# The first batch's third product: from four tile products to one product of seven blocks

## The chip, the cores and the metric

The kernel runs on one core of one Trainium2 chip. The metric is the device time of one execution in microseconds (us); the median over several runs is compared. The core's engines work side by side, each through its own instructions in order: TensorE (PE, matrix products into PSUM; PEld is its loading of the stationary operand), VectorE (DVE), ScalarE (ACT), GpSimd (POOL) and SyncE (SP), whose queue here issues nearly all DMAs. An instruction waits at the head of its engine's queue until what it needs is done, and everything behind it waits too.

## The reference, cut to what matters

The whole is one transformer block over 4 batches of 512 tokens of width 512: a layer norm, then attention and a mixture of experts on the normalised rows, both added to the input. The change touches only the shared expert, which every token passes through:

```python
def _expert_ffn(x, w1, wg, w2):
    return jax.nn.silu(x @ w1) * (x @ wg) @ w2
output = _expert_ffn(x, Ws1, Wsg, Ws2)
...
x = L0_attn_x
xn = _layernorm(x, axis=-1)
x = x + _L0_attn_ref(xn, ...) + _L0_ffn_ref(xn, ...)
```

All three matrices are 512 x 512 in float32. For one batch each product is a 512 x 512 by 512 x 512 product. The third one, by Ws2, is the one that the change does in another way, and only for the first batch.

## The kernel before, in words

**Order.** A planner places instructions on each engine. Those wrapped in `keep(...)` stay in the order in which the program writes them, engine by engine; the others are placed where the planner's own estimate of time finds them ready, the earlier written one first. Nearly all of TensorE's and VectorE's work in this stretch is kept. The sums of weight blocks on POOL (`gadd`, `gsub`, L959 and L962) and the additions of `product_y` (L868) are not.

**Loads.** SyncE loads a 128-token tile of x, Ws1, a second tile, Wsg, the third and fourth tile, Ws2, and then the four tiles of the second batch. The tiles go into `acc`, which also collects the result. `wbuf` holds the three matrices.

**The first batch** is done tile by tile, so that work can begin on the first 128 tokens. `norm(g, 1)` normalises a tile on VectorE (with one square root on ScalarE); POOL copies it into another layout (`xp`, L495), SyncE stores that to `xn_d` in DRAM (L501); TensorE transposes it and ScalarE copies it into `xnT` (L524, L525). Then `ffn_in` (L142) multiplies by Ws1 (tile h) and by Wsg (tile g), ScalarE takes Silu of h (L153), VectorE multiplies by g (L157, `at_s`), and `ffn_out` (L164) multiplies by Ws2 in four matmuls of 512 columns (`y_s`), which VectorE adds to `acc` (L828).

Between h and g of a tile, `between` writes work for later: for tiles 1 and 2 the transpose of the next tile and the normalisation of batch 1 or 2 as a whole: statistics, four scalings (L499), four stores to `xn_d`, and, behind them on SyncE's queue, four loads back in turned order (`xq`, L511). For tile 3 it is the statistics of batch 3 and `turn_batch(1)`, four transposes on VectorE from `xq` into `xnT` (L519). All of it is kept, so on VectorE it stands ahead of the tile's own multiplication at L157. `y_s` of a tile is written behind h and g of the following tile; that of the last tile is a hook behind the third product of `product_h("s1")`.

**The other batches** use seven products of blocks in place of eight. `seven` (L230) takes 2 x 2 blocks of both operands; `first_factors` and `second_factors` form four sums of one operand's blocks each, so that seven products (four matmuls of 256 columns each) suffice. They run in ORDER 0, 1, 5, 4, 6, 2, 3 into three PSUM banks. After products 0, 5, 4 and 6 ScalarE copies a bank out (L297); the others are read from the bank. `product_h` and `product_g` do the first two products of a batch, `product_y` the third, whose seven parts are added to `acc` by POOL (copied ones) and VectorE (banks). A `hooks` entry is called behind the product of that number. `tokens(b)` gives a batch's four sums from `xnT` on VectorE (L841) in parts; `feature_factors` and `weight_factors` give those of the matrices, on POOL here. The fourth sum of each set is written over a block of the matrix itself, so it waits for the last reader of that block.

**Around the change** the order written is: four tiles; POOL's sums of Ws1; the token sums of batch 1; the scaling of batch 3; `turn_batch(2)`; `product_h("s1")` with the last tile's third product inside; POOL's sums of Wsg and Ws2; `turn_batch(3)`; `product_g("s1")` with the start of the routing; and so on.

Of the kernel before, what the change touches and what calls it, by code (L numbers as in the profile page):

```python
# [10 lines left out]
F32 = mybir.dt.float32  # L11
# [7 lines left out]
P = 128  # L19
B, S, D = 4, 512, 512  # L20
NT = B * S
NTT = NT // P
TPB = S // P
# [4 lines left out]
FC = FF // P  # L28
# [14 lines left out]
def kernel(  # L43
# [38 lines left out]
    nc = tc.nc  # L82
    keep = tc.keep_in_program_order
# [15 lines left out]
    acc = const.tile([P, NTT, D], F32, tag="acc", name="acc")  # L99
    xnT = const.tile([P, DC, NT], F32, tag="xnT", name="xnT")  # L100
# [19 lines left out]
    sw = moe.enter_context(tc.tile_pool(name="sw", bufs=1, side="right"))  # L120
# [10 lines left out]
    def rows(src):  # L131
        return src.rearrange("(c p) f -> p c f", p=P)

    def ffn_in(at, name, w, x_of, between, step=FC):

        hp = fps.tile([P, S], F32, tag="h", name=f"h_{name}")
        gp = fps.tile([P, S], F32, tag="g", name=f"g_{name}")
        for ps, wt in ((hp, w[0]), (gp, w[1])):
            for f in range(FC):
                for c in range(DC):  # L140
                    keep(
                        nc.tensor.matmul(  # L142
                            ps[:, ts(f, P)],
                            wt[:, c, ts(f, P)],
                            x_of(c),
                            start=(c == 0),
                            stop=(c == DC - 1),
                        )
                    )
            if ps is hp:  # L150
                between()
        sl = sw.tile([P, S], F32, tag="v", name=f"sl_{name}", bufs=5)
        keep(nc.scalar.activation(sl, hp, AF.Silu))  # L153
        cols = [t.rearrange("p (c n) -> p c n", c=FC) for t in (gp, sl)]

        for f in range(0, FC, step):
            keep(nc.vector.tensor_mul(*(t[:, f : f + step] for t in (at, *cols))))  # L157
        return at

    def ffn_out(name, at_t, w, fix=lambda ins: None):  # L160
        yp = fps.tile([P, D], F32, tag="y", name=f"y_{name}")
        for f in range(FC):
            fix(
                nc.tensor.matmul(  # L164
                    yp, at_t[:, f, :], w[2][:, f, :], start=(f == 0), stop=(f == FC - 1)
                )
            )
        return yp
# [39 lines left out]
    def first_factors(add, sub, a11, a12, a21, a22, s1, s2, s4, s3):  # L208
        add(s1, a21, a22)
        sub(s2, s1, a11)  # L210
        sub(s4, a12, s2)
        sub(s3, a11, a21)
        return a11, a12, s4, a22, s1, s2, s3

    def second_factors(sub, b11, b12, b21, b22, t1, t2, t4, t3):
        sub(t1, b12, b11)
        sub(t2, b22, t1)
        sub(t4, b21, t2)
        sub(t3, b22, b12)
        return b11, b21, b22, t4, t1, t2, t3  # L220
# [49 lines left out]
    V, G = nc.vector, nc.gpsimd  # L270

    def block(t):
        if len(t.shape) > 2:
            axes = " ".join("abc"[: len(t.shape) - 1])
            t = t.rearrange(f"p {axes} -> p ({axes})")
        return t.rearrange("p (j f) -> p j f", j=2)

    def blocks(t):

        return [[t[:, 2 * k : 2 * k + 2, half[n]] for n in range(2)] for k in range(2)]  # L280
# [7 lines left out]
    def product(name, tag, a, w, done, hooks):  # L288

        banks = banks_of(tag, name)

        def kept(i, k):
            t = sw.tile([P, D], F32, tag="v", name=f"v{i}_{name}", bufs=5)
            keep(nc.scalar.copy(block(t), banks[k]))  # L297
            return block(t)

        copies = {0: (1, 0), 5: (2, 0), 4: (5, 2), 6: (3, 0)}  # L300
        sums = {1: 1, 2: 2, 3: 0}

        def then(p):
            if p in copies:
                done(copies[p][0], kept(*copies[p]))
            else:
                done(-p, banks[sums[p]])
            if p in hooks:
                hooks[p]()

        seven(a, w, banks, then, keep)

    def product_h(name, at, a, w, hooks={}, fix=lambda ins: None, more=G):

        (c11, c12), (c21, c22) = blocks(at)
        v = {}

        def silu(*blocks):
            for c in blocks:
                keep(nc.scalar.activation(c, c, AF.Silu))  # L320

        def done(i, src):
            v[i] = src
            if i == -1:
                fix(V.tensor_add(c11, src, v[1]))
            elif i == 3:
                silu(c11)
                fix(more.tensor_add(c22, v[3], v[5]))
            elif i == -2:
                fix(V.tensor_add(c12, src, v[2]))  # L330
            elif i == -3:
                silu(c12, c22)
                keep(nc.scalar.activation(c21, src, AF.Silu))

        product(f"h{name}", "h", a, w, done, hooks)
# [28 lines left out]
    def act_tile(name):  # L364
        return sw.tile([P, FC, S], F32, tag="at", name=f"at_{name}")

    def feature_factors(i, add, sub):

        (a11, a21), (a12, a22) = blocks(wbuf[i])
        return first_factors(add, sub, a11, a12, a21, a22, *wsum[i], a21)  # L370

    def weight_factors(sub):
        (b11, b12), (b21, b22) = blocks(wbuf[2])
        return second_factors(sub, b11, b12, b21, b22, *wsum[2], b12)
# [72 lines left out]
    with tc.tile_pool(name="rt", bufs=1) as rt, tc.tile_pool(name="fwork", bufs=2) as fw:  # L447
# [4 lines left out]
        def load_x(g):  # L452
            keep(nc.sync.dma_start(acc[:, g, :], x_f[ts(g, P), :]))
# [366 lines left out]
        shared = wbuf  # L820

        def shared_in(g, between):
            at = fw.tile([P, FC, P], F32, tag="at1", name=f"at_s{g}")
            return ffn_in(at, f"s{g}", shared, lambda c: xnT[:, c, ts(g, P)], between)

        def shared_out(g, at, fix=lambda ins: None):
            yp = ffn_out(f"s{g}", at, shared, fix)
            fix(nc.vector.tensor_add(acc[:, g, :], yp, acc[:, g, :]))  # L828

        def tokens(b):  # L830

# [22 lines left out]
        def parts_of(b):  # L854
            it = tokens(b)
            return lambda: next(it)

        def product_y(b, a, w, hooks={}, fix=lambda ins: None):
            def c(t, n):
                g = b * TPB + 2 * t  # L860
                return acc[:, g : g + 2, half[n]]

            to = {1: c(0, 0), -1: c(0, 0), 2: c(0, 1), -2: c(0, 1)}
            to.update({5: c(1, 1), 3: c(1, 1), -3: c(1, 0)})

            def done(i, src):
                eng = G if i > 0 else V
                fix(eng.tensor_add(to[i], src, to[i]))  # L868

            product(f"ys{b}", "y", a, w, done, hooks)  # L870

        def load(dst, src):
            keep(nc.sync.dma_start(dst, src))
# [3 lines left out]
        load(shared[0], rows(ws1))  # L877
        load_x(1)
        load(shared[1], rows(wsg))
        load_x(2)  # L880
        load_x(3)
        load(shared[2], rows(ws2))
        for g in range(TPB, 2 * TPB):
            load_x(g)


        warm = fps.tile([P, TPB, P], F32, tag="y", name="warm")
# [12 lines left out]
        for t, n, step, mul in (  # L900
# [3 lines left out]
                t, pattern=[[step, n]], base=S if t is by512 else 0, channel_multiplier=mul,  # L904
# [33 lines left out]
        def between():  # L938
            if t + 1 < TPB:
                turn_x(t + 1, tiles[t + 1])  # L940
                xq[t] = norm(t * TPB, TPB)
            else:
                stats[3] = statistics(3 * TPB, TPB)
                turn_batch(1, xq.pop(1))

        stats = {}
        at, xq = None, {}
        for t in range(TPB):
            nxt = shared_in(t, between if t else between_0)
            if at is not None:  # L950
                shared_out(t - 1, at, keep)
            at = nxt
        parts = routing()

        def route():
# [5 lines left out]
        def gsub(*t):  # L961
            return G.tensor_sub(*t)  # L962

        fs_h = feature_factors(0, gadd, gsub)
        x_of = parts_of(1)
        x_of()
        x_of()
        x1 = x_of()
        xq[3] = scaled(3 * TPB, TPB, *stats[3])
        turn_batch(2, xq.pop(2))  # L970
        last_tile = lambda: shared_out(TPB - 1, at, keep)
        at_1 = act_tile("s1")
        product_h("s1", at_1, fs_h, x1, {5: last_tile})
        fs_g = feature_factors(1, gadd, gsub)
        fs_y = weight_factors(gsub)
        turn_batch(3, xq.pop(3))
        for s in range(SURE, NUNIT):
            to = y_d[ts(s, S), :].rearrange("(t p) (c f) -> p t c f", p=P, f=P)
# [2 lines left out]
        x_of = parts_of(2)  # L981
# [11 lines left out]
        x_of = parts_of(3)  # L993
# [386 lines left out]
    with tc.If(used < SURE + 1) as few:  # L1380
        at = act_tile("few").rearrange("p c (t f) -> p t c f", t=TPB)[:, 0]
        at = ffn_in(at, "few", wbuf, lambda c: xT[SURE][:, c, :P], nothing, 1)
        y = sw.tile([P, D], F32, tag="v", name="y_few", bufs=5)
        yp = ffn_out("few", at, wbuf, keep)
# [395 lines left out]
```

## Time and profile before

| | us |
|---|---|
| median of 14 runs | 1340.39 |
| lowest and highest | 1339.82, 1342.11 |
| the profiled execution's own time | 1340.54 |
| its span in the profile | 1338.8 |
| TensorE busy | 1329.6 |
| VectorE busy | 971.3 |
| POOL busy | 847.4 |
| ScalarE busy | 405.8 |

Times in the profile are counted from the start of the span. A row of the timeline has the start, the length, the engine, the line of the kernel, the operation, what is written and read, and the count; in brackets the engine's idle time ahead of it and what ended that. `P` is 128. A matmul of float32 stands in the rows as two records, so a group of four matmuls has x8. The stretch that the change touches is roughly the first 70 us of the span.

### The profile page before, as it was taken

Reading aid. Unit: us, or ns where it says so; the run is one execution under the profiler, and the core shown is the slowest. Engines: PE = TensorE matmul, PEld = TensorE weight load, DVE = VectorE, ACT = ScalarE, POOL = GpSimd, SP = SyncE. Lnnn points to the kernel's source line nnn. Section 1 sums busy time; section 2 is a strip of 40 time slices with the busy share of each in tenths; the row PEclk is TensorE's granted clock in tenths of the full one; section 3 lists DMA queues with packets and bytes.
Section 4 is the critical chain, followed back from the end, with each engine's and each line's share of the span. In section 5 each row is a group of like instructions: output and inputs, shape, how many; then the busy total and the mean of one; then the engine's idle time right before and its main releaser. Section 6 shows DMA issues by size and latency. Waiting matters only on the chain.

```text
span 1338.8 us, 17913 instructions
## 1 busy us (share of the span) xinstructions
PE 1329.6 (99%) x5949; PEld 993.9 (74%) x5949; DVE 971.3 (73%) x1426; ACT 405.8 (30%) x714; POOL 847.4 (63%) x952
## 2 busy tenths in 40 slices
PE   9999999999999999999999999999999999999998
PEld 8778888888888888877655666667666666666676
DVE  7669486676767677676458679877788777897775
ACT  3333222322223322212223423323333323233231
POOL 5113664564545465532277789888898888988883
PEclk9999999999999999999999999999999999999999
DMA  7850356866667675523401331243322333213332
GB/s 280 191 159 19 93 134 158 220 180 185 186 169 203 165 228 162 157 92 98 147 16 45 110 111 32 89 132 110 110 60 69 124 111 110 76 58 120 110 110 87
DMA packets 174100, 167.90 MB, mean 125 GB/s; under 512 B 57904, under 2 KB 136752, under 8 KB 174000
## 3 DMA queue, kind: packets, MB, share of 16 engines
q1 hardware_dynamic: 161264, 133.10, 34.1%
q0 software_dynamic: 12736, 33.57, 8.7%
q8 instruction: 49, 0.80, 0.3%
q14 instruction: 51, 0.42, 0.1%
HBM read 116.02 MB, written 34.87 MB: 113 GB/s over the span
## 4 chain that ended last, share of the span: by engine, by line
PE 96%; DVE 2%; ACT 1%; DMA 0%; issue 0%; SPq 0%; POOL 0%; DVEq 0%; ACTq 0%; POOLq 0%
PE op L230 15%; PE hr L230 11%; PE av L1513 11%; PE yr L230 11%; PE gr L230 9%; PE sb L1432 4%; PE sa L1432 4%; PE pq L1297 4%; PE gs L230 3%; PE sa L1443 3%; PE ys L230 2%; PE pqr L1282 2%; PE hs L230 2%; PE sb L1443 2%; PE sb L1532 2%; PE h_s L142 1%
## 5 line engine op out<-in xcount | busy, mean ns | idle before, releaser
L182 POOL DMA_INDIRECT xs<-xn_d,idx_i x208 | 230.0, 1106 | 193.7 <-DVE xT L199 134.6
L1469 POOL TENSOR_TENSOR pt<-pt,tri 128x128 f32<-128x128 f32 x256 | 139.6, 566 | 68.9 <-ACT pt L1465 62.2
L1465 ACT ACTIVATE pt<-pt 128x512 f32<-128x512 f32 x160 | 94.4, 628 | 257.9 <-DVE pt L1461 256.9
L1513 PEld LDWEIGHTS av<-pt,xnT 128*128 128x128 f32 x512 | 95.5, 190 | 83.6 <-issue 47.7
L1513 PE MATMUL av<-pt,xnT 128*128 128x512 f32 (+3 forms) x512 | 149.8, 436 | 0.0
L230 PE MATMUL op<-m,og 128*128 128x256 f32 x512 | 118.6, 380 | 0.5 <-DVE og L1566 0.5
L1271 DVE TENSOR_TENSOR swap_q<-qraw,sinT 32x512 f32<-32x512 f32 x128 | 117.7, 919 | 1.7
L1497 POOL TENSOR_TENSOR su<-su,pt 128x256 f32<-128x256 f32 (+1 forms) x128 | 105.2, 822 | 10.0
L230 PEld LDWEIGHTS op<-m,og 128*128 128x128 f32 x512 | 96.1, 190 | 14.4 <-DVE og L1566 1.3
L1461 DVE TENSOR_SCALAR pt<-sa 128x512 f32<-128x512 f32 x64 | 41.1, 682 | 70.7 <-PE sa L1443 70.7
L1664 POOL DMA_INDIRECT yg<-y_d,pos_i x48 | 54.4, 1134 | 56.7 <-issue 50.3
L230 PE MATMUL op<-m,s 128*128 128x256 f32 x384 | 88.2, 379 | 0.1
L1497 POOL TENSOR_TENSOR su<-pt 128x384 f32<-128x384 f32 x64 | 83.8, 1310 | 0.0
L1612 POOL TENSOR_TENSOR acc<-acc,v 128x512 f32<-128x512 f32 x60 | 80.6, 1344 | 5.1 <-ACT v L1605 3.2
L230 PEld LDWEIGHTS op<-m,s 128*128 128x128 f32 x384 | 73.0, 190 | 10.2 <-issue 0.5
L1677 DVE SCALAR_TENSOR_TENSOR acc<-yg,wk,acc 128x512 f32<-128x512 f32 x48 | 56.7, 1181 | 19.1 <-POOL acc L1612 17.9
L1605 ACT COPY v<-op 128x512 f32<-128x512 f32 x64 | 37.5, 585 | 108.3 <-PE op L230 107.1
L1566 DVE TENSOR_TENSOR og<-og,rb 128x512 f32<-128x512 f32 (+1 forms) x68 | 68.5, 1068 | 0.6 <-PE rb L1552 0.2
L1615 DVE TENSOR_TENSOR acc<-op,acc 128x512 f32<-128x512 f32 x48 | 31.7, 686 | 49.5 <-POOL acc L1612 47.3
L230 PE MATMUL yr<-w,at_r 128*128 128x256 f32 x288 | 67.1, 381 | 0.5 <-DVE at_r L351 0.2
L230 PE MATMUL gr<-xT,w 128*128 128x256 f32 x288 | 66.1, 379 | 0.0
L230 PE MATMUL hr<-xT,w 128*128 128x256 f32 x288 | 66.1, 379 | 0.0
(339 smaller groups left out, 2809.4 us busy)
## 6 DMA issues: line engine op xcount, KB each, us to landing
m<-m_d SPq DMA_DIRECT2D x112, 256.0 KB, 5.9
w<-in_L_ffn_W_dram SPq DMA_DIRECT2D x52, 512.0 KB, 4.2
rb<-rc SPq DMA_DIRECT2D x240, 64.0 KB, 2.0
w<-in_L_ffn_Wg_dram SPq DMA_DIRECT2D x26, 512.0 KB, 4.1
y_d<-v_yr SPq DMA_DIRECT2D x36, 256.0 KB, 2.3
y_d<-none SPq DMA_DIRECT2D x24, 256.0 KB, 5.0
acc<-in_L_attn_x_dram SPq DMA_DIRECT2D x16, 256.0 KB, 6.7
xn_d<-xp SPq DMA_DIRECT2D x16, 256.0 KB, 3.5
```

Source lines behind the costliest of these rows:

```text
L182: nc.gpsimd.indirect_dma_start(out=xs[blk][:, q, :], out_offset=None, in_=xn_d[:, :], in_offset=bass.IndirectOffsetOnAxis(ap=idx_i[:, q, b ...
L230: nc.tensor.matmul(banks[k][:, t, :], a[p][:, j, ts(t, P)], b[p][:, j, :], start=(k not in used), stop=(t == j == 1), skip_group_check=True,)
L1271: keep(nc.vector.tensor_mul(swap[there, :], raw[here, :], tables[1][here, :]))
L1432: nc.tensor.matmul(where(j, kc), lat(b, 1)[:, ts(kc, P)], qc[j][:, kc * P :], start=(kc != 3), stop=False,)
L1443: nc.tensor.matmul(where(j, kc), lat(b, 2)[r, ts(kc, P)], qr[r, kc * P :], start=False, stop=(kc != 1),)
L1465: keep(nc.scalar.activation(t, t, AF.Exp, scale=QK_SCALE))
L1469: keep(nc.gpsimd.tensor_mul(m, m, tri))
L1497: nc.gpsimd.tensor_add(t[:, kc * P :], prev, pt[:, PT[j, kc] : PT[j, kc] + PT_W[kc]])
L1513: nc.tensor.matmul(av[:, kc * P :], lat(b, 3)[:, ts(kc, P)], pt[:, PT[j, kc] : PT[j, kc] + PT_W[kc]], start=(kc == 0), stop=(kc == TPB - 1),)
L1566: keep(nc.vector.tensor_mul(o[:, j, cols], o[:, j, cols], rb[:, cols]))
L1612: keep(eng.tensor_add(block, block, v))
L1677: nc.vector.scalar_tensor_tensor(acc[:, g, :], yg, wk[:, g, k : k + 1], acc[:, g, :], ALU.mult, ALU.add)
```

## The change

The third product of the first batch is no longer done tile by tile. The four tiles write their activations into one tile `at_0` of the whole batch, and `ffn_out` isn't called for them. Behind the four tiles, the four sums of `at_0`'s blocks are formed on VectorE, and `product_y(0, ...)` does the third product as seven products of blocks, as for the other batches. The sums of Ws2's blocks (`fs_y`) are written ahead of those of Ws1, and the parts of batch 1's token sums hang on hooks of `product_y(0)`. `product_h("s1")` has no hook any more. On SyncE's queue Ws2 is loaded behind the four tiles of the second batch instead of ahead of them.

```diff
         def shared_in(g, between):
-            at = fw.tile([P, FC, P], F32, tag="at1", name=f"at_s{g}")
-            return ffn_in(at, f"s{g}", shared, lambda c: xnT[:, c, ts(g, P)], between)
-
-        def shared_out(g, at, fix=lambda ins: None):
-            yp = ffn_out(f"s{g}", at, shared, fix)
-            fix(nc.vector.tensor_add(acc[:, g, :], yp, acc[:, g, :]))
+            at = at_0[:, :, ts(g, P)]
+            ffn_in(at, f"s{g}", shared, lambda c: xnT[:, c, ts(g, P)], between)
...
-        load_x(2)
-        load_x(3)
+        for g in range(2, 2 * TPB):
+            load_x(g)
         load(shared[2], rows(ws2))
-        for g in range(TPB, 2 * TPB):
-            load_x(g)
...
-        stats = {}
-        at, xq = None, {}
+        stats, xq = {}, {}
+        at_0 = fw.tile([P, FC, S], F32, tag="at2", name="at_s0", bufs=1)
         for t in range(TPB):
-            nxt = shared_in(t, between if t else between_0)
-            if at is not None:
-                shared_out(t - 1, at, keep)
-            at = nxt
+            shared_in(t, between if t else between_0)
...
+        fs_y = weight_factors(gsub)
+        (c11, c12), (c21, c22) = blocks(at_0)
+        x = [block(sw.tile([P, S], F32, tag=f"as{i}", name=f"as{i}_s0")) for i in (1, 2, 4)]
+        as_0 = first_factors(
+            lambda *t: keep(V.tensor_add(*t)),
+            lambda *t: keep(V.tensor_sub(*t)),
+            c11, c21, c12, c22, *x, c12,
+        )
+        x_of = parts_of(1)
+        product_y(0, as_0, fs_y, {5: x_of, 4: x_of})
+        x1 = x_of()
         fs_h = feature_factors(0, gadd, gsub)
-        x_of = parts_of(1)
-        x_of()
-        x_of()
-        x1 = x_of()
         xq[3] = scaled(3 * TPB, TPB, *stats[3])
         turn_batch(2, xq.pop(2))
-        last_tile = lambda: shared_out(TPB - 1, at, keep)
         at_1 = act_tile("s1")
-        product_h("s1", at_1, fs_h, x1, {5: last_tile})
+        product_h("s1", at_1, fs_h, x1)
         fs_g = feature_factors(1, gadd, gsub)
-        fs_y = weight_factors(gsub)
         turn_batch(3, xq.pop(3))
```

## The prediction

> **What bounds the kernel now.** I read the page's busy shares and its chain first, then what TensorE waited for (us in total, times, longest).
>
> ```profile
> PE 1329.6 (99%) x5949; PEld 993.9 (74%) x5949; DVE 971.3 (73%) x1426; ACT 405.8 (30%) x714; POOL 847.4 (63%) x952
> ...
> PE 96%; DVE 2%; ACT 1%; DMA 0%; issue 0%; SPq 0%; POOL 0%; DVEq 0%; ACTq 0%; POOLq 0%
> ...
> PE warm L889 <- POOL ident masks.py:199: 1.5, 1, 1.5
> PE sa L1432 <- DVE y_few L1386: 1.0, 1, 1.0
> ```
>
> TensorE is busy 99% of the span and carries 96% of the chain; once started, its longest single wait is 1.0 us. So matmul time removed is time won, and any new wait of TensorE is paid in full, unless a later wait shrinks by as much. There is hardly any later wait to shrink. Next the chain in order of time, around the change (start, length, what):
>
> ```profile
> 34.53 3.44 PE y_s L164 x8
> 37.97 3.57 PE h_s L142 x32
> 41.54 3.57 PE g_s L142 x32
> 45.12 3.44 PE y_s L164 x8
> 48.55 5.18 PE hs L230 x24
> 53.73 3.43 PE y_s L164 x8
> 57.16 6.91 PE hs L230 x32
> 64.07 6.91 PE gs L230 x32
> ...
> 106.01 12.09 PE gs L230 x56
> ```
>
> TensorE goes through here without a gap. The four groups y_s (23.52, 34.53, 45.12, 53.73) do more than multiply: each stands between a tile's work on other engines and the matmuls that need it. The timeline of VectorE shows what they stand in front of:
>
> ```profile
> 35.27 1.91 DVE L499 TENSOR_SCALAR xp<-acc,mv,rs 128x512 f32<-128x512 f32 x4
> 37.10 0.68 DVE L157 TENSOR_TENSOR at_s<-g_s,sl_s 128x512 f32<-128x512 f32 x1
> ...
> 43.09 2.49 DVE L519 STREAM_TRANSPOSE xnT<-xq 128x512 f32<-128x512 f32 x4 [0.61 <-DMA xq<-xn_d]
> 45.99 0.69 DVE L157 TENSOR_TENSOR at_s<-g_s,sl_s 128x512 f32<-128x512 f32 x1 [0.41 <-ACT sl_s L153]
> ...
> 49.20 0.68 DVE L841 TENSOR_TENSOR xt<-xnT 128x512 f32<-128x512 f32 x1
> 49.91 0.69 DVE L841 TENSOR_TENSOR xt<-xnT,xt 128x512 f32<-128x512 f32 x1
> ```
>
> The reader is to see the last tile's product at_s at 45.99. In VectorE's kept order it stands behind the four transposes of batch 1, and those wait for a DMA (xq) that landed at 43.09. It doesn't matter today: its matmuls run at 53.73.
>
> **The change part by part.**
>
> *Matmuls.* Removed: four y_s groups, 4 x 3.44 = 13.75 us. Added: a product of seven, 56 records, 12.09 us by the last row of the chain above. Sum: -1.66 us, all on TensorE's path. This is the whole gain to be had, 0.12%.
>
> *Where TensorE arrives.* y_s of tiles 0 and 1 leave the stretch ahead of the last tile's gate matmuls, which now end at 45.12 - 2 x 3.44 = 38.24. Of the seven products, the first two (ORDER 0, 1) take at_0's blocks c11 and c21, the tokens of tiles 0 and 1, finished by 30; they run to 38.24 + 2 x 1.727 = 41.69. The third (5) takes s2 = c12 + c22 - c11, which needs tiles 2 and 3.
>
> *The new wait.* Going earlier on TensorE moves nothing on VectorE: the transposes wait for xq, whose chain has no matmul in it. SyncE's queue shows it:
>
> ```profile
> 23.20 3.77 SPq L453 DMA_DIRECT2D acc<-in_L_attn_x_dram  x8
> ...
> 28.64 2.96 SPq L501 DMA_DIRECT2D xn_d<-xp  x4
> 35.74 1.92 SPq L511 DMA_DIRECT2D xq<-xn_d  x4
> ```
>
> Those loads stand behind the xn_d stores of batch 0, which wait for POOL's last copy at 22.19; then the stores, the loads back, 43.09. So transposes 43.09 to 45.58; at_s of tile 3 to 46.3 (its Silu ends by 45 or earlier, as two acc additions leave VectorE's queue ahead of it); s1 to 47.0 and s2 to 47.7 at 0.7 each, the spacing of the dependent pair at 49.20 and 49.91; matmuls some 0.1 later, 47.8. TensorE waits 47.8 - 41.69 = 6.1 us. Queued behind that wait are all of TensorE's later instructions, product_h of batch 1 first. The term is +6.1.
>
> *The wait's bounds.* ws2 moves on SyncE's queue behind four 256 KB loads. Its factors are sums on POOL, which stand among the copies that gate the chain:
>
> ```profile
> 14.26 2.49 POOL L962 TENSOR_TENSOR f<-w,f 128x512 f32<-128x512 f32 x2
> 16.71 1.45 POOL L962 TENSOR_TENSOR f<-w 128x512 f32<-128x512 f32 x1
> 18.11 0.60 POOL L495 COPY xp<-xn 128x512 f32<-128x512 f32 x1
> 18.68 2.61 POOL L962 TENSOR_TENSOR f<-w,f 128x512 f32<-128x512 f32 x2
> 21.24 0.60 POOL L495 COPY xp<-xn 128x512 f32<-128x512 f32 x1
> 22.19 0.61 POOL L495 COPY xp<-xn 128x512 f32<-128x512 f32 x1 [0.34 <-DVE xn L494]
> ```
>
> The DMA engines are full until about 17.4, so ws2 lands by then instead of before 16.7. These sums are not kept, and the planner may set them anew. If all three go behind the copies, VectorE loses two small operations that stood 1.20 and 1.13 beside POOL instead of 0.16, and 0.2 of the next: all is 2.2 earlier, wait 3.9. If the fourth sum (written over the matrix, at 55.53 today because the last y_s read it) comes early too, ahead of the copies, all is 1.27 later. One addition acc += bank, also unkept, ahead of s1 costs 0.7. Ends: 3.9 and 6.1 + 1.3 + 0.7 = 8.1; I keep 6.1, the order as it is.
>
> *The clock after the wait.* No row shows TensorE after a wait of six microseconds. The nearest rows are a wait of 1.0 without effect, and the start:
>
> ```profile
> L889 PE MATMUL warm<-ident x26: 275/421/582, 1.5 to 6.7; 128*128 128x128 f32 x26
> ```
>
> There 26 records took 5.50 us (1.48 to 6.98); 32 records of the same shape take 3.57 in h_s, so 26 would take 2.90. The start was slow by 2.60, though the page's PEclk has 9 in every slice. The ends are 0 and +2.6. A 6.1 us stop is nearer to the idle start than to 1.0 us; I take +2.0, a little under that end since TensorE has been idle for less long.
>
> The Trainium skill (TensorE: Matmul & The Clock Gate, section "Why this matters for your kernels") warns of gaps above about 3 us between matmuls, after which the clock falls to half, and gives about 3.4 us of work to get it back; this speaks against the change. By that rule the term would be about 1.7, an estimate from the page's 3.4; by the granted clock of the profile alone, 1.00 even while the warm-up matmuls ran slowly, it would be 0.
>
> *The other edits, at no cost.* VectorE: four additions of y_s go, three additions and four sums of activations come, +3 x 0.7 = 2.1 us. The four token sums (49.20), scaled and turn_batch(2) now follow s1 to s3 and end at about 58; their first user, the third product of product_h, comes at 56.4 + 3.45 = 59.9. Cover 1.9 us; without it a late microsecond costs one. ScalarE: four copies of 0.58, one after each of the products 0, 5, 4, 6; the copy of product 0 stands behind the last Silu (45 at the latest) and must leave its bank before product 5, at 47.8: cover 2.2. POOL: four additions of 1.27, 5.1 us in 12 of product_y. They can hold VectorE's s1 and s2 if they run at the same time: the multiplication of two SBUF operands at 79.64 took 1.27 instead of 0.69 beside POOL. The first ends at about 46, before s1; cover 0.3, and 0.6 if it is gone, inside the range. SyncE: loads of batch 1 rows come earlier, which no wait shows to be wanted; scaled(3)'s stores shift by some 0.3 and xq(3) is used at 68.97 without a wait. product_h loses its hook, so its own third product is no longer given 3.43 us of cover, but the whole product_y now stands ahead of its sums.
>
> *Sum.* -1.66 + 6.1 + 2.0 = +6.44. The wait is not given back: behind product_h, TensorE's stretch up to 160 us has one wait of 0.42. The profiled execution took 1340.54 (span 1338.8 and 1.74 around it), 0.15 above the median of 1340.39. So 1340.4 + 6.5 = 1346.9. A measurement of this kernel tells about 0.2% (2.7 us) from no change.
>
> **The rivals.**
>
> *A, the forecast: the stop of about 6 us and a slow restart.* 1346.9. Chance 0.45.
>
> *B, the same stop, no slow restart.* For it: 1.00 in every slice of the clock's row. Against: the start. 1340.4 + 4.5 = 1344.9. Chance 0.27.
>
> *C, POOL's sums of ws2 set behind the copies.* For it: ws2 arrives later, so a planner may find them ready later. Against: the copies at 18.11 and 21.24 were themselves late behind sums, and the fourth sum may now come early too. Wait 3.9, little or no slow restart: 1340.4 - 1.66 + 3.9 = 1342.6, in effect no change. Chance 0.15.
>
> *D, products 0 and 1 wait as well,* if the dependence of at_0 is judged by a span that takes in tile 3's slices. Wait from 38.24 to 46.4, 8.2, then no stop at product 5: -1.66 + 8.2 + 2.6 = +9.1, 1349.5. Against: batch 1's transposes wrote xnT at 43.09 while g_s read other columns of it until 45.12, so slices are told apart. Chance 0.08.
>
> *E, faster: no stop.* The mechanism is one: xq lands before TensorE gets there. From 47.8 to 41.69 it must come 6.1 us earlier, at 37.0; at 38.6 (4.45 earlier) the change breaks even. Full gain: 1340.4 - 1.66 = 1338.7, within 0.2% even so; 0.2% faster needs another microsecond from nowhere that the profile shows. Against: the last normalised tile itself is ready only at 22.12, and POOL copies it 0.1 later; no reordering on POOL gives more than 2.2. The same result would come if at_s stood ahead of the transposes; but at_s of tile 0 ran at 22.05, behind tile 3's normalisation, with both its inputs ready by 20.3, so the written order holds. Chance 0.05.
>
> **How the numbers follow.** A and B are slower by over 0.2% (0.72), and so is D (0.08): 0.80. C, and most of E, lie within: 0.17. Faster: 0.03. The range leaves out half of D and E and the lower end of C: from 1342.0, somewhat under C's 1342.6, to 1350.5, which is A with the fourth sum ahead of the copies (+1.3), an addition ahead of s1 (+0.7), the full 2.6 (+0.6) and a microsecond for VectorE's cover running out.
>
> **What would show it.** Right: no y_s groups; ys at 38 with two products of 3.45, then TensorE idle some 6 us with DVE as_s as the releaser; at_s of tile 3 behind transposes that start at about 43; the first product after the stop at more than 1.73 us; gs of batch 1 starting at about 70.5 instead of 64.07, and from there the same distances as before. Wrong: transposes at 41 or sooner (C), products 0 and 1 behind the stop (D), no idle time (E), or the lost time given back before 160 us. If POOL's ws2 sums hold up the copies of xp more than 1.3 us, the result is above my range.

## The result and the profile after

The changed kernel takes 1353.18 us (median of 6 runs, 1352.39 to 1354.72) against 1340.5 for the kernel before: a ratio of 1.0095, 95% interval 1.0085 to 1.0105. The direction was forecast, the size was not: 12.7 us more instead of 6.5, and above the range, which ended at 1350.5. The profiled execution has a span of 1352.5 and took 1354.73.

From the page of the changed kernel, the clock granted to TensorE (PEclk: one digit for each of 40 slices of the span, in tenths of full speed), and the longest of TensorE's waits (us in total, times, longest):

```profile
PEclk9799999999999999999999999999999999999999
...
PE ys L230 <- DVE as_s L961: 13.5, 1, 13.5
```

One wait is new, of 13.5 us in the second slice, and the granted clock is low in the same slice. The timeline of TensorE shows the wait and the slow matmuls behind it:

```profile
8.03 3.84 PE L142 MATMUL h_s<-xnT,w 128*128 128x128 f32 x32 [0.68 <-ACT xnT L525]
...
38.03 3.62 PE L230 MATMUL ys<-w,at_s 128*128 128x256 f32 x16
55.14 5.60 PE L230 MATMUL ys<-f,as_s 128*128 128x256 f32 x16 [13.49 <-DVE as_s L961]
60.59 1.89 PE L230 MATMUL ys<-w,at_s 128*128 128x256 f32 x8
...
77.85 3.62 PE L230 MATMUL gs<-xnT,w 128*128 128x256 f32 x16
```

In the kernel before, the same stretch began and ended so:

```profile
8.09 3.84 PE L142 MATMUL h_s<-xnT,w 128*128 128x128 f32 x32 [0.67 <-ACT xnT L525]
...
63.91 3.62 PE L230 MATMUL gs<-xnT,w 128*128 128x256 f32 x16
```

The first two products start at 38.03, as forecast (38.24), then TensorE stands. The third and fourth start at 55.14, not at 47.8, and take 60.59 - 55.14 = 5.45 us, where two such products take 3.45. The stretch from the first h_s matmul to the first gs of batch 1 is 77.85 - 8.03 = 69.82 us; before it was 63.91 - 8.09 = 55.82. It is 14.0 longer in this execution, and from there the same distances follow: the routing's lgT comes 7.00 behind gs in both. So the whole difference is made in this stretch. Its terms are -1.66 of matmuls, +13.5 of waiting and +2.0 of slow matmuls, together 13.8. This execution took 1.5 more than the median.

Why did the wait last until 55.14? VectorE's timeline of the changed kernel (line numbers differ a little between the kernels; L837 here is L841 before):

```profile
48.93 0.69 DVE L864 TENSOR_TENSOR acc<-ys,acc 128x512 f32<-128x512 f32 x1 [5.33 <-POOL acc L864]
49.54 2.48 DVE L519 STREAM_TRANSPOSE xnT<-xq 128x512 f32<-128x512 f32 x4
51.94 0.65 DVE L157 TENSOR_TENSOR at_s<-g_s,sl_s 128x512 f32<-128x512 f32 x1
52.52 0.67 DVE L837 TENSOR_TENSOR xt<-xnT 128x512 f32<-128x512 f32 x1
53.11 0.69 DVE L960 TENSOR_TENSOR as_s<-at_s 128x512 f32<-128x512 f32 x1
53.71 0.69 DVE L837 TENSOR_TENSOR xt<-xnT,xt 128x512 f32<-128x512 f32 x1
54.31 0.69 DVE L961 TENSOR_TENSOR as_s<-as_s,at_s 128x512 f32<-128x512 f32 x1
```

Three things differ from the forecast's order. An addition of `product_y(0)` (L864, acc += bank) stands ahead of the transposes of batch 1 and holds VectorE idle for 5.33 us. Two token sums (L837) stand between the last tile's at_s and the sums of activations that TensorE waits for. And all is later from the start, as SyncE's queue shows:

```profile
25.54 5.60 SPq L453 DMA_DIRECT2D acc<-in_L_attn_x_dram  x8
...
38.41 1.92 SPq L511 DMA_DIRECT2D xq<-xn_d  x4
```

It issues its eight loads at 25.54 instead of 23.20, and those of xq at 38.41 instead of 35.74.

The addition's wait is a chain over three engines. The chain that ended last, in order of time:

```profile
43.43 0.18 DVE ve L469
...
44.97 0.21 ACT sd L471
...
46.48 0.60 ACT sl_s L153
47.08 0.48 ACT v_ys L297
...
47.64 1.27 POOL acc L864
```

The addition adds to a block that POOL adds to first; POOL waits for ScalarE's copy of the first product; that copy stands behind the last Silu, which stands behind the square root of batch 3, with two table loads. None of it is needed by the transposes.

On POOL, which sets the lateness, two of Ws2's sums, the first and the fourth, and the last copy that gates the DMA chain:

```profile
18.79 1.27 POOL L953 TENSOR_TENSOR f<-w 128x512 f32<-128x512 f32 x1 [1.23 <-DMA w<-in_L_ffn_Ws_dram]
...
23.33 1.27 POOL L953 TENSOR_TENSOR w<-w 128x512 f32<-128x512 f32 x1
24.54 0.60 POOL L495 COPY xp<-xn 128x512 f32<-128x512 f32 x1
```

POOL waits 1.23 us for Ws2, whose load landed at 18.71, and the fourth sum (w<-w, at 55.53 before) now runs ahead of the last copy, which moves from 22.19 to 24.54.

### The profile page after: what moved, and what is told of

It is laid out like the page before. It is cut to its first block, busy times and chain, and to the rows that moved or that the text cites. A ratio compares the mean times of both kernels' runs of the same rounds, so it can differ in the third digit from the quotient of the medians.

```text
span 1352.5 us, 17980 instructions
## 1 busy us (share of the span) xinstructions
PE 1329.2 (98%) x5973; PEld 998.7 (74%) x5973; DVE 974.7 (72%) x1429; ACT 408.1 (30%) x718; POOL 852.5 (63%) x956
## 4 chain that ended last, share of the span: by engine, by line
PE 94%; DMA 2%; DVE 2%; ACT 1%; POOL 1%; issue 0%; SPq 0%; DVEq 0%; ACTq 0%; POOLq 0%
PE op L230 14%; PE hr L230 11%; PE yr L230 11%; PE av L1510 10%; PE gr L230 10%; PE sb L1429 4%; PE sa L1429 4%; PE pq L1294 4%; PE ys L230 3%; PE gs L230 3%; PE sa L1440 3%; PE pqr L1279 2%; PE hs L230 2%; PE sb L1440 2%; PE sb L1529 2%; PE pj_cq L1237 1%
```

## The experiments

The table gives the stretch from the first h_s matmul to the first gs of batch 1, read from each profile, since little else is in it. Experiments 1 to 4 ran on a chip on which the kernel before itself took 1398.3 us, and 8, 10 and 11 on one on which it took 1394.9; there the times scattered more, so the ratios are wide and the stretch is the better reading. Each stretch is that of one execution, the profiled one.

| | stretch | stop | third and fourth product | ratio to before (95%) |
|---|---|---|---|---|
| before | 55.82 | none | | 1 |
| changed | 69.82 | 13.49 | 5.45 | 1.0095 (1.0085 to 1.0105) |
| 1 additions in written order | 64.00 | 8.08 | 5.05 | 1.0059 (1.0025 to 1.0094) |
| 2 Ws2 early | 67.77 | 11.98 | 4.91 | 1.0080 (1.0051 to 1.0108) |
| 3 TensorE kept at work | 67.69 | 1.25 | 3.53 | 1.0095 (1.0051 to 1.0139) |
| 4 both 1 and 2 | 64.60 | 8.76 | 4.95 | 1.0065 (1.0029 to 1.0102) |
| 9 the forecast's order | 64.05 | 6.61 | 6.56 | 1.0057 (1.0041 to 1.0072) |
| 5 Ws2's sums behind the copies | 61.89 | 5.34 | 5.66 | 1.0056 (1.0041 to 1.0071) |
| 6 transposes later | 54.17 | none | 3.45 | 0.9993 (0.9984 to 1.0003) |
| 7 the same, Ws2 early | 54.17 | none | 3.46 | 0.9993 (0.9984 to 1.0002) |
| 8 before, Ws2 late | 55.82 | none | | 1.0008 (0.9971 to 1.0044) |
| 10 as 3, 12 products | 67.93 | 3.22 | 3.52 | one execution |
| 11 as 3, 10 products | 69.10 | 4.70 | 4.92 | one execution |

**1. The additions in the written order.**

```diff
-        product_y(0, as_0, fs_y, {5: x_of, 4: x_of})
+        product_y(0, as_0, fs_y, {5: x_of, 4: x_of}, keep)
```

> product_y(0)'s seven additions in the written order, nothing else. Theory: the stop of 13.5 us is lateness of the DMA chain (2.7), plus an addition that the planner set ahead of batch 1's transposes (3.8), plus token sums that slipped between the sums of activations (1.0), plus the 6.1 forecast. Kept, the additions go behind these sums: transposes start at 45.8, when xq lands, the stop is 8.7, the restart still slow by 2.0, and the time is 1353.2 - 4.8 = 1348.4. Rival: the transposes could not have started much before 49.5 anyway, since xq landed only then; then only the 1.0 of the token sums comes back: 1352.2.

VectorE's timeline, then the first row of TensorE behind the stop:

```profile
44.89 2.49 DVE L519 STREAM_TRANSPOSE xnT<-xq 128x512 f32<-128x512 f32 x4 [3.19 <-DMA xq<-xn_d]
47.30 0.65 DVE L157 TENSOR_TENSOR at_s<-g_s,sl_s 128x512 f32<-128x512 f32 x1
...
48.71 0.69 DVE L961 TENSOR_TENSOR as_s<-as_s,at_s 128x512 f32<-128x512 f32 x1
...
49.55 5.21 PE L230 MATMUL ys<-f,as_s 128*128 128x256 f32 x16 [8.08 <-DVE as_s L961]
```

The transposes wait for xq again and start at 44.89; the token sums are gone from between; the stretch is 5.8 shorter. The stop itself is 5.4 shorter. Of this about 0.8 is due to the loads of xq, issued at 37.47 instead of 38.41 in an execution that was 0.2 ahead throughout; the addition and the token sums behind it cost the other 4.6. The rival that xq landed only at 49 falls. The token sums came loose with the addition: each kept instruction is pinned behind the one written just ahead of it on its engine, and the token sums had an addition that wasn't kept just ahead of them.

**2. Ws2 loaded as before.**

```diff
-        for g in range(2, 2 * TPB):
-            load_x(g)
+        load_x(2)
+        load_x(3)
         load(shared[2], rows(ws2))
+        for g in range(TPB, 2 * TPB):
+            load_x(g)
```

> The loads in the order of the kernel before (Ws2 ahead of the second batch's rows), the rest as changed. Theory: POOL no longer waits 1.2 us for Ws2, but the fourth sum of Ws2 is still free to run ahead of POOL's last copies (1.27); the last copy ends near 23.8 instead of 25.1, everything behind is 1.3 earlier: 1351.9. Rival 1: the place of the load makes the whole lateness, 2.7: 1350.5. Rival 2: the addition ahead of the transposes hangs on ScalarE, not on this chain: 1353.2.

POOL no longer waits; its last copy ends at 23.67 instead of 25.14, although the fourth sum still stands ahead of it, and the stop is 1.5 shorter, near the 1.3 expected. The rest of the 2.1 us by which the stretch is shorter is a restart that is 0.5 less slow.

**3. TensorE kept at work in the gap.** The added products' result is read by nobody; nothing else is changed.

```diff
+        dummy = fps.tile([P, S], F32, tag="h", name="dummy")
+        def busy():
+            for _ in range(14):
+                keep(nc.tensor.matmul(dummy, ident, xnT[:, 0, :S], start=True, stop=True))
-        product_y(0, as_0, fs_y, {5: x_of, 4: x_of})
+        product_y(0, as_0, fs_y, {1: busy, 5: x_of, 4: x_of})
```

> Fourteen products of 512 columns of the identity, 12.0 us in all, are put on TensorE between the second and the third product of product_y(0), into a bank that nobody reads; all other queues stay in the order of the changed kernel. Theory: the third and fourth product run at half speed because TensorE stood idle, so with work in the gap they take 3.45 instead of 5.45 and the kernel 1353.2 - 2.0 = 1351.2. Rival: they are slow because of their operands or of what runs beside them: 1353.2, and 5.45 again.

```profile
41.33 12.18 PE L969 MATMUL dummy<-xnT,ident 128*128 128x512 f32 x28
54.76 3.69 PE L230 MATMUL ys<-f,as_s 128*128 128x256 f32 x16 [1.25 <-DVE as_s L961]
```

The next row starts at 58.29, so the two products take 3.53 instead of 5.45, with the same operands: the slow restart comes from standing still. The stretch is 2.1 shorter; the whole time, on that chip, doesn't show it.

**10 and 11. How long a stop is too long.** The same with 12 and 10 of the added products (range(12), range(10)).

> The kernel with the products of the identity in the gap, 12 instead of 14 of them: TensorE stands still for about 3.0 us instead of 1.25. Theory: half speed needs a standstill longer than this; the third and fourth product take 3.5 us, as after 1.25. Rival: three microseconds are enough, and they take 5 to 6.

> The same with 10 products: a standstill of about 4.7 us. Theory: this is enough in some executions or all, as 5.3 was; the third and fourth product take 5 to 6.6 us. Rival: below 5 us nothing happens, 3.5.

The first row is of 10, the second of 11:

```profile
54.87 3.69 PE L230 MATMUL ys<-f,as_s 128*128 128x256 f32 x16 [3.22 <-DVE as_s L961]
...
55.21 5.09 PE L230 MATMUL ys<-f,as_s 128*128 128x256 f32 x16 [4.70 <-DVE as_s L961]
```

After 3.22 us the two products take 3.52 (the next row starts at 58.39), after 4.70 they take 4.92 (60.13). Each is a single execution, 1403.07 and 1414.20 us, and these times tell nothing about 2 us. Nor do the two give a limit for the length of a stop: in experiment 9 the clock fell 2.50 us after the last matmul, as the section on the prediction shows.

**4. Both 1 and 2.**

> Both edits at once: additions in the written order, Ws2 loaded as before. Theory: they add up, -4.8 and -1.3: the stop is 7.4, transposes at 44.4, 1347.1. Rival: one makes the other worthless, because both end at the same wait (ScalarE's last Silu, at 47.1 in the changed kernel, at 46.0 before): then at_s of the last tile starts no earlier than about 47, the stop is 8 or more and the time 1347.8 or above.

The stretch is 5.2 shorter than the changed kernel's, not more than with 1 alone (5.8). Here neither account was quite right: at_s started at 47.05, directly behind the transposes, which began at 44.63, and Silu, which ended at 46.83, was nearly as late. On SyncE one small load (gb) took 2.46 us to issue instead of 0.50, so xq came as late as in experiment 1; and s1 took 1.45 instead of 0.69 beside POOL's first addition. One execution with such an issue says little on whether the two edits add up. Experiment 9 answers that better.

**9. The forecast's own order.** Edits 1 and 2, and the fourth sum of Ws2 behind POOL's last copy of xp (`last_xp[0]` is that copy):

```diff
+        def sum_of(*t):
+            mine = nullcontext() if len(made) < 3 else tc.issue_after(last_xp[0].ins)
+            with mine:
+                made.append(G.tensor_sub(*t))
+        made = []
-        fs_y = weight_factors(gsub)
+        fs_y = weight_factors(sum_of)
```

> The changed kernel with the three things put right that the forecast had assumed: additions in the written order, Ws2 loaded ahead of the second batch's rows, and the fourth sum of Ws2 behind POOL's last copy, so that POOL's order up to there is that of the kernel before. Theory: now the forecast's own sum holds: transposes at 43.1, the stop 6.1, the third and fourth product 1.5 to 2.0 slow, in all -1.66 + 6.1 + 1.7 = 6.1 above before, a ratio of 1.0046. Rival: ScalarE's Silu of the last tile (behind the square root of batch 3) sets at_s, whatever the transposes do; then at_s starts at 47, the stop is 7.5 or more and the ratio 1.0056.

VectorE, then TensorE:

```profile
43.13 2.49 DVE L523 STREAM_TRANSPOSE xnT<-xq 128x512 f32<-128x512 f32 x4 [1.30 <-DMA xq<-xn_d]
45.55 0.66 DVE L157 TENSOR_TENSOR at_s<-g_s,sl_s 128x512 f32<-128x512 f32 x1
46.24 1.45 DVE L972 TENSOR_TENSOR as_s<-at_s 128x512 f32<-128x512 f32 x1
...
48.56 6.72 PE L230 MATMUL ys<-f,as_s 128*128 128x256 f32 x16 [6.61 <-DVE as_s L973]
55.12 1.89 PE L230 MATMUL ys<-w,at_s 128*128 128x256 f32 x8
```

With the assumed order restored, the forecast's dates return one by one: transposes 43.13 (43.09), at_s 45.55 (45.6), stop 6.61 (6.1). The half microsecond is s1, 1.45 instead of 0.7 beside POOL's addition at 45.88. The restart cost 6.56 - 3.45 = 3.1, more than 2.0 and more than the 2.6 that had been its upper end. The stretch is 8.2 above before, and its terms give -1.66 + 6.6 + 3.1 = 8.05. The median time, 1348.45, is 8.0 above before; that it agrees so well is in part chance, since the profiled execution took 1350.44 and had two short waits of TensorE far behind the stretch (0.7 and 0.4 us). The rival with Silu at 47 falls: it ended at 45.33.

**5. All sums of Ws2 behind the copies** (edit 1 kept, the load late):

```diff
-        fs_y = weight_factors(gsub)
+        with tc.issue_after(last_xp[0].ins):
+            fs_y = weight_factors(gsub)
```

> Additions in the written order; Ws2 loaded late, as changed; all four sums of Ws2 behind POOL's last copy of xp. Theory (the forecast's rival C): without these sums beside it VectorE is 2.2 us earlier, transposes at 40.9, the stop 3.9, and a stop so short slows the restart by 0.5 at most: 2.2 to 2.7 above before, 1.0018. Rival: the chain is earlier but at_s then waits for ScalarE's Silu, which hangs on the statistics of batch 3 and ends at about 45: the stop stays near 5.5, the restart is slow, 5.5 above before, 1.0041.

VectorE's at_s of the last tile:

```profile
41.46 2.49 DVE L523 STREAM_TRANSPOSE xnT<-xq 128x512 f32<-128x512 f32 x4 [0.57 <-DMA xq<-xn_d]
44.41 0.69 DVE L157 TENSOR_TENSOR at_s<-g_s,sl_s 128x512 f32<-128x512 f32 x1 [0.46 <-ACT sl_s L153]
```

The rival was right. The chain is earlier, with the transposes at 41.46, but at_s now waits for Silu, and s1 takes 1.60 beside POOL; the stop is 5.34, not 3.9, and the restart slow by 2.2. So case C's 3.9 us, with little or no slow restart, wasn't to be had by this order.

**6 and 7. Nothing ahead of the last tile's multiplication.** The statistics of batch 3 and the transposes of batch 1 leave `between` of tile 3 and become hooks of `product_y(0)`, kept; the square root goes behind ScalarE's last copy. 7 also loads Ws2 early, as in experiment 2. The computation is complete.

```diff
-            else:
-                stats[3] = statistics(3 * TPB, TPB)
-                turn_batch(1, xq.pop(1))
...
-        product_y(0, as_0, fs_y, {5: x_of, 4: x_of})
+        hooks = {1: count, 5: turn_and_sums, 4: x_of, 6: root}
+        product_y(0, as_0, fs_y, hooks, keep)
```

Here `count` does the statistics without the square root, `turn_and_sums` calls `turn_batch(1)` and `x_of`, and `root` takes the square root.

> The changed kernel with the statistics of batch 3 and the transposes of batch 1 written behind the last tile's multiplication and the four sums of activations, the square root behind the last copy of product_y(0), and the additions in the written order. Ws2 is loaded late. Theory: nothing stands between the last gate matmul and at_s any more, the third product is ready at about 41, TensorE does not stop, and the time is 1.66 below before, 1338.8, a ratio of 0.9988. Rival: the transposes are now the last thing that product_h of batch 1 waits for: they start at 46 or later (xq lands at about 45) and end at 48.5, so 1.7 us of cover is left; if that is not so, TensorE stops there by what they are late, and the ratio is above 1.

> The same with Ws2 loaded ahead of the second batch's rows. Theory: no stop of TensorE, xq some 1.3 us earlier than in the kernel with the late load, the same time, 1338.8, a ratio of 0.9988. Rival: the place of the load matters even without the stop (a later wait for the routing's transposes): then this one is faster than the kernel with the late load by a microsecond or more.

TensorE in experiment 7, whose first two products start at 37.74:

```profile
41.19 3.62 PE L230 MATMUL ys<-f,as_s 128*128 128x256 f32 x16
...
61.91 3.62 PE L230 MATMUL gs<-xnT,w 128*128 128x256 f32 x16
```

There is no stop and no slow restart, and the stretch is 54.17, which is 1.65 below before: the -1.66 of the forecast's first term. The whole times, 1339.10 (experiment 6) and 1339.31 (7) against 1340.46, are lower by a microsecond, but the intervals take in 1, so a gain of this size isn't shown by the times. The place of Ws2's load makes no difference once nothing waits.

**8. The load order alone, in the kernel before** (the edit of 2, reversed).

> The kernel before with one part of the change alone: Ws2 loaded behind the second batch's rows. Theory: POOL's sums of Ws2 wait for it as in the changed kernel and the chain to the transposes of batch 1 is 1.3 to 2.7 later, but there 2.8 us of cover lie behind it (transposes done at 45.6, product_h of batch 1 at 48.4, TensorE busy with the third tile's y_s in between), so the time is that of the kernel before, ratio 1.000 within 0.001. Rival: the first tile's y_s at 23.4 or product_h of batch 1 now waits, and the load order alone costs 1 to 3 us, ratio 1.001 to 1.002.

The stretch is 55.82, as without the edit. But the chain was hardly later: POOL found Ws2 there and didn't wait, and xq's loads were issued at 36.23 instead of 35.74, not 1.3 to 2.7 later. So the run shows that TensorE takes no notice of half a microsecond; the cover of 2.8 wasn't put to use.

## Why the prediction was wrong

- **Matmuls, -1.66:** right. Experiments 6 and 7 show it alone, as -1.65.
- **Where TensorE arrives:** right; the first two products ran without waiting, 38.03 to 41.65. Case D, that they wait too, didn't happen.
- **The new wait:** right in kind and place, wrong in size, 13.49 instead of 6.1. With the order that the forecast had assumed it is 6.61 (experiment 9). The rest comes from the next two items: 6.1 + 2.7 (the loads of xq issued later) + 4.6 = 13.4.
- **The wait's bounds** is the step that failed. "One addition acc += bank, also unkept, ahead of s1 costs 0.7" priced the addition by its duration, as if it could only stand directly ahead of s1. It stood ahead of the transposes and waited: VectorE stood for 5.33 us, and the two token sums that had been pinned behind it slipped in ahead of s1 and s2. Experiment 1 puts the two at 4.6 us together, in place of 0.7. This alone is more than the 3.6 us between the forecast and the end of its range.
- **POOL's sums:** the fourth sum came ahead of the last copy, +1.27, as bounded; POOL's wait for Ws2 came on top, and the copy was 2.35 later in all. The forecast let Ws2 land by about 17.4; it landed at 18.71, and a wait of POOL for it had no price in the sum, though the prediction's last sentence names such a hold-up as what would put the result above the range. Experiment 2 gives back 1.5 of it.
- **The clock:** right in kind; that the +2.0 is also what the changed kernel paid is luck, since experiment 9, whose stop is the one forecast, paid 3.1, above the upper end of 2.6. The granted clock (stretch and length, PE's busy time, granted clock, DMA) fell in the gap and came back under work, in the changed kernel:

```profile
44.00:45.00 1.00, 0.00 (x0) 1.00 1.29 189
45.00:46.00 1.00, 0.00 (x0) 0.68 0.99 319
46.00:47.00 1.00, 0.00 (x0) 0.50 1.06 408
...
58.00:59.00 1.00, 1.00 (x4) 0.50 0.00 0
59.00:60.00 1.00, 1.00 (x6) 0.99 0.00 0
```

  The last matmul ended at 41.65; the clock fell to half at 45.37 and came back at 59.02, 3.88 us after work began. The 13.65 us between are four times 3.41, and so it is throughout: in all 13 traces the stretches of full and of half clock are whole multiples of 3.41 us, but for the last of each, which the end of the record cuts off. Experiment 9 (first five rows) and experiment 10 (the other two), one row for each step of 3.41 us:

```profile
41.04:44.45 3.41, 0.91 (x5) 1.00 1.11 312
44.45:47.86 3.41, 0.00 (x0) 0.50 0.42 130
47.86:51.28 3.42, 2.72 (x7) 0.50 1.18 186
51.28:54.69 3.41, 3.41 (x10) 0.50 0.25 34
54.69:58.10 3.41, 3.41 (x17) 1.00 0.02 5
...
49.61:53.02 3.41, 2.04 (x5) 1.00 1.21 213
53.02:56.43 3.41, 1.56 (x7) 1.00 0.46 67
```

  In experiment 9, 0.91 us of work in a step was too little to keep the clock, and 2.72 too little to bring it back, so the restart at 48.56 stayed slow until 54.69. In experiment 10 the stop of 3.22 us lay across two steps, each with 1.56 us of work or more, and the clock stayed. In experiment 2 a step with 2.80 us of work brought it back.

  In all seven runs with a slow restart, the extra time is half of what lies between the restart and the step back, to within 0.1 us: 3.88 us gave 2.0 in the changed kernel, 6.13 gave 3.1 in experiment 9, 2.84 gave 1.5 in experiment 11. So the price is set by where the restart falls between two steps, not by the length of the stop, and the forecast's "a little under that end since TensorE has been idle for less long" has no support. Nor has the reading of 1.00 at the start: in the kernel before, the first record of the clock is the step to full at 6.38, where the warm-up matmuls go from 0.21 us apart to 0.11, and the profile shows 1.00 where it has no record.

  The Trainium skill (TensorE: Matmul & The Clock Gate, Part 1) says that the window of about 3.4 us, the figure that the prediction quotes, runs freely, so that the moment of the change depends on where work falls in it; these traces show the same, with steps of 3.41 us and extra times from 1.5 to 3.1. Its rule of about 3 us for a gap (section "Why this matters for your kernels") is not a limit here: 2.50 us without work were enough in experiment 9, and 3.22 were not in experiment 10.
- **The other edits, at no cost:** mostly right. The cover of 0.3 for s1 beside POOL's addition was gone in experiments 4, 5 and 9, at 0.75 to 0.9 each, where the forecast gave 0.6.
- **Case C** was wrong in a way the forecast hadn't seen: with the chain 2.2 earlier (counted from the first h_s matmul), Silu becomes the last thing that at_s waits for (experiment 5).
- **Not given back later:** right; the distances behind gs are those of before.

## What to carry to other kernels

When a change moves a block of matmuls ahead, ask what each of its operands is queued behind on the other engines, not only when it could be computed; here the last tile's multiplication stood behind work of other batches that nobody had needed early. An instruction left to the planner can be placed ahead of a wait, and its price is then that wait and everything pinned behind it, not its own duration; in a stretch ordered by hand, one free instruction loosens the ones written behind it too. Once the order is written so that nothing waits, the 1.65 us of saved matmuls appear in full, and so does their smallness against a stop of TensorE, which costs its length and, once the granted clock has stepped down, another 1.5 to 3.1 us here.

## What the runs showed of the hardware

The granted clock of TensorE changed only between 1.00 and 0.50, and in steps of 3.41 us. It stayed at 1.00 through a stop of 3.22 us (experiment 10) and fell in every stop of 4.70 us or more, in experiment 9 already 2.50 us after the last matmul. The slow time afterwards doesn't grow with the stop (2.0 us lost after 13.49, 3.1 after 6.61, 1.5 after 8.76). An addition or subtraction of two SBUF operands on VectorE took 1.45 to 1.76 us instead of 0.69 when it started while a POOL addition ran (experiments 4, 5, 6, 7 and 9), and each time it ended 0.54 to 0.56 us after POOL's. A small load of 3.5 KB (gb) took about 0.5 us to issue on SyncE's queue in most executions, 1.03 and 1.28 in experiments 8 and 11, and 2.46 in experiment 4, where the chain of DMAs behind it moved with it; what caused that is open.
